# Weights loaded in three parts between the first pairs' x, gate weights in separate tiles: a four-layer graph network on one core

## The chip, the cores and the metric

The kernel runs on one core of one Trainium2 chip. The metric is the device time of one execution in microseconds. Of the kernel before there are six runs: median 1531.78 us, from 1530.32 to 1532.71.

## The reference, cut to what matters

64 graphs of 256 nodes with 128 features go through four layers, each closed by a residual and a layer norm. All is float32. Layer 0, where the change lies, is a gated recurrent unit with five steps:

```python
def step(h, _):
    m_in = jnp.einsum('nm,bmd->bnd', in_matrix, h)
    m_out = jnp.einsum('nm,bmd->bnd', out_matrix, h)
    av = jnp.concatenate([m_in, m_out], axis=-1)
    u3 = h @ u3_w.T + u3_b
    z = jax.nn.sigmoid(av @ w3_w.T + w3_b + u3)
    r = jax.nn.sigmoid(av @ w4_w.T + w4_b + u3)
    hv = jnp.tanh(av @ w5_w.T + w5_b + (r * h @ u5_w.T + u5_b))
    h = (1.0 - z) * h + z * hv
    return (h, None)
...
x = _layernorm(x + _L0_gnn_ref(x, adj, adj, ..., 5), axis=-1)
```

`in_matrix` and `out_matrix` are both `adj`, so the two halves of each gate weight act on the same message and can be added once. The three later layers are an attention over edges that depends on weights only, a graph attention with an isomorphism network, and a Chebyshev filter of order 3.

## The kernel before, in words

The 64 graphs are worked on as 32 pairs. A pair's x is a tile of 128 partitions by 512 columns with nodes on the partitions (class X, 13 buffers); its transpose hT comes from a second array, xT (class T, 3 buffers). The pairs do not depend on each other, so that many are in work at the same time.

One step of layer 0 (`layer0`, L571) is: the **spread**, adjacency times h (`spread`, L484, four matmuls of 256 columns into one bank of PSUM), copied to SBUF (L200); the **reset** gate, u3 times hT (L578) plus w4 times the message (L579), its tanh on ScalarE (L582) and r times h on VectorE (L584); the **z** gate, w3-w4 times the message added onto the same bank (L586), its tanh (L588); the **candidate**, w5 times the message (L593) and u5 times r times h (L594), its tanh (L596); and three VectorE operations for the new h (L598 to L601). The new hT is turned back to nodes on partitions by `turn`: a 32x32 block transpose on VectorE (L465), a store to DRAM on SP's queue (L467) and four reads (L473). A float32 matmul appears in the trace as two records.

The order of all work is set by a planner, `Schedule.order`. It knows for each operation an engine, a duration and how long after its end the result can be used: `seen`, plus LAG, 0.8 us. It takes again and again the operation that could start first, and on equal starts the one that is due first. Then all instructions are issued in that order. Each engine executes its own instructions in that order, and SP issues all DMAs in it. So a wrong figure in the plan doesn't make the kernel wrong; it makes an instruction stand in the queue and wait.

Loads are operations of SP without inputs. `load` (L225) gives each 0.45 us on SP and `seen` of 1.7 + KB/256 us. At the start the loads are, in this order: aT, x0, W0 (the eight matrices of layer 0, 512 KB), hT0, the bias columns, x1, hT1, x2, hT2, the adjacency a, W1 (13 further matrices, 832 KB), the rows. The x and hT of pairs 3 to 31 are added in the loop over pairs; the x go out as soon as one of 13 buffers is free, an hT needs one of 3.

Four matmuls on ones (L253) stand ahead of the first spread. VectorE then adds the halves of the three gate weights into one tile, w345, subtracts w4 from w3 (L260) and halves u5 (L261). The dependencies are kept per tile: whatever reads w345 waits for all writers of w345.

Of the kernel before, what the change touches and what calls it, by code (L numbers as in the profile page):

```python
# [12 lines left out]
P = 128  # L13
N = 256
D = 128
# [8 lines left out]
NEG_MASK = 3.0e38  # L24
NEG_ADJ = 9.0e15

MATS = ["w3a", "w3b", "w4a", "w4b", "w5a", "w5b", "u3", "u5",
        "l1w0", "l1w1", "wp", "wpT", "w1", "w2",
        "v0", "v1", "v2", "v3", "v4", "v5", "v6"]
N_L0 = 8  # L30
COLS = ["w3_b", "u3_b", "w4_b", "w5_b", "u5_b", "bp", "a_src", "a_dst", "mlp_g", "mlp_b", "e0", "e1"]
ROWS = ["l1_bias", "bp", "b1", "gat_g", "gat_b", "b2"]

# [13 lines left out]
def mm(cols):  # L47

    return cols * 0.00168 + 0.005
# [117 lines left out]
def kernel(ctx: ExitStack, tc: tile.TileContext, x, xT, adj, adjT, mats, cols, rows, out):  # L167
    nc = tc.nc
# [5 lines left out]
    S = Schedule(n_pairs)  # L174

    def fixed(shape, name):
        return Value(ap=const.tile([P, *shape], F32, name=name), name=name)

    def pe(us, fn, r, w):
        S.add([("PE", us, fn)], r, w)  # L180

    def act(us, fn, r, w):
        S.add([("ACT", us, fn)], r, w)

    def dve(us, fn, r, w):
        S.add([("DVE", us, fn)], r, w)

    def dve2(us, fn, r, w):
        S.add([("DVE+", us, fn)], r, w)
# [13 lines left out]

    diff, ident = fixed([P], "diff"), fixed([P], "ident")
    aT, a = fixed([2, N], "aT"), fixed([2, N], "a")
    W0, W1 = fixed([N_L0, D], "W0"), fixed([len(MATS) - N_L0, D], "W1")
    ccol = fixed([len(COLS)], "ccol")
    n_rows = len(ROWS) * D + 2
    rbc = fixed([n_rows], "rbc")
# [1 line left out]

    def mat(name):
        i = MATS.index(name)
        return W0.ap[:, i, :] if i < N_L0 else W1.ap[:, i - N_L0, :]

    def col(name):
        i = COLS.index(name)
# [2 lines left out]
    def row(name, n):  # L220
        i = ROWS.index(name)
        return rbc.ap[:, None, i * D:(i + 1) * D].to_broadcast([P, n, D])

    def load(o, i, v, kb=256):
        S.add([("SP", 0.45, lambda: nc.sync.dma_start(o(), i))], [], [v], 1.7 + kb / 256)  # L225

    xs = [Value("X", name=f"x{p}") for p in range(n_pairs)]
    hTs = [Value("T", name=f"hT{p}") for p in range(n_pairs)]

    def load_x(p):  # L230
        load(lambda: xs[p].at(4, D), x[2 * p:2 * p + 2].rearrange("b (t p) d -> p (b t) d", p=P), xs[p])
        load(lambda: hTs[p].at(2, N), xT[2 * p:2 * p + 2].rearrange("b d n -> d b n"), hTs[p])

    pool(1.0, lambda: nc.gpsimd.iota(diff.ap, pattern=[[1, P]], base=0, channel_multiplier=-1,
# [1 line left out]
    dve(0.2, lambda: nc.vector.tensor_scalar(ident.ap, diff.ap, 0.0, None, op0=ALU.is_equal), [diff], [ident])  # L236
    dve(0.1, lambda: nc.vector.memset(neg_half.ap, -0.5), [], [neg_half])
    load(lambda: aT.ap, adjT.rearrange("(t p) i -> p t i", p=P), aT)
    load(lambda: xs[0].at(4, D), x[0:2].rearrange("b (t p) d -> p (b t) d", p=P), xs[0])
    load(lambda: W0.ap, mats[:, :N_L0], W0, 512)  # L240
    load(lambda: hTs[0].at(2, N), xT[0:2].rearrange("b d n -> d b n"), hTs[0])
    load(lambda: ccol.ap, cols, ccol, 16)
    for p in range(1, 3):
        load_x(p)
    load(lambda: a.ap, adj.rearrange("(t p) j -> p t j", p=P), a)
    load(lambda: W1.ap, mats[:, N_L0:], W1, 832)
    load(lambda: rbc.ap, bass.AP(tensor=rows.tensor, offset=rows.offset, ap=[[0, P], [1, n_rows]]), rbc)


# [4 lines left out]

    w345, u5h, bzrh = fixed([3, D], "w345"), fixed([D], "u5h"), fixed([3], "bzrh")
    for i, w in ((1, "w4"), (0, "w3"), (2, "w5")):
        dve(0.25, lambda i=i, w=w: nc.vector.tensor_add(w345.ap[:, i, :], mat(w + "a"), mat(w + "b")), [W0], [w345])
    dve(0.25, lambda: nc.vector.tensor_sub(w345.ap[:, 0, :], w345.ap[:, 0, :], w345.ap[:, 1, :]), [w345], [w345])  # L260
    dve(0.2, lambda: nc.vector.tensor_scalar(u5h.ap, mat("u5"), 0.5, None, op0=ALU.mult), [W0], [u5h])  # L261
    for i, (b, c) in enumerate((("w3_b", "u3_b"), ("w4_b", "u3_b"), ("w5_b", "u5_b"))):
        dve(0.16, lambda i=i, b=b, c=c: nc.vector.tensor_add(bzrh.ap[:, i:i + 1], col(b), col(c)), [ccol], [bzrh])
# [4 lines left out]
    def centre(v, ap, k):  # L268

        m = Value("S", name="mean")  # L270
        mean = lambda: m.at(32)[:, :k]
        dve(0.15 * k + 0.1, lambda: nc.vector.tensor_reduce(mean(), ap(), AX.X, ALU.add), [v], [m])
        dve(0.1, lambda: nc.vector.tensor_scalar(mean(), mean(), -1.0 / D, None, op0=ALU.mult), [m], [m])
        dve(0.15 * k + 0.1, lambda: nc.vector.tensor_add(ap(), ap(), mean().unsqueeze(2).to_broadcast([P, k, D])), [m, v], [v])
# [97 lines left out]
    dve(TT, lambda: nc.vector.tensor_copy(offT.ap, t5.at(2, N)), [t5], [offT])  # L372


    i_w = MATS.index("l1w0") - N_L0
    assert MATS[i_w + N_L0:i_w + N_L0 + 3] == ["l1w0", "l1w1", "wp"] and ROWS[:3] == ["l1_bias", "bp", "b1"]
    centre(W1, lambda: W1.ap[:, i_w:i_w + 3, :], 3)
    i_w1 = MATS.index("w1") - N_L0
    centre(W1, lambda: W1.ap[:, i_w1:i_w1 + 1, :], 1)
    centre(rbc, lambda: rbc.ap[:, :3 * D].rearrange("p (k d) -> p k d", d=D), 3)  # L380
    maskb, ginT, eps1 = fixed([2, N], "maskb"), fixed([2, N], "ginT"), fixed([1], "eps1")
# [60 lines left out]
    def to_sbuf(t, name):  # L442
        v = Value("A", name=name)
        evacuate(lambda: v.at(512), lambda: t.at(512), [t], [v])
        return v
# [32 lines left out]
    def spread(i, right):  # L478

        t = Value("PS", name="ps")  # L480
        for b in range(2):
            def fn(b=b):
                for j in range(2):
                    nc.tensor.matmul(t.at(2, N)[:, b, :], tokens(i)[:, 2 * b + j, :], right.ap[:, j, :],  # L484
                                     start=(j == 0), stop=(j == 1))
            pe(mm(512), fn, [i, right], [t])
        return t
# [35 lines left out]
    def layer_norm(y, o):  # L523
        normalize(y, o, *stats(y))
# [46 lines left out]
    def layer0(x0, hT):  # L571
        h = x0
        for s in range(STEPS):
            mT = to_sbuf(spread(h, aT), "mT")
            t = Value("PS", name="ps")

            def reset(t=t, hT=hT, mT=mT):
                nc.tensor.matmul(t.at(512), mat("u3"), hT.at(512), start=True, stop=False)  # L578
                nc.tensor.matmul(t.at(512), w345.ap[:, 1, :], mT.at(512), start=False, stop=True)  # L579
            pe(mm(1024), reset, [W0, w345, hT, mT], [t])  # L580
            r, z, hv, new = (Value("A", name=n) for n in ("r", "z", "hv", "hT"))
            act(0.59, lambda t=t, r=r: nc.scalar.activation(r.at(512), t.at(512), AF.Tanh, bias=bzrh.ap[:, 1:2], scale=0.5),  # L582
                [t, bzrh], [r])
            dve2(TT, lambda r=r, hT=hT: nc.vector.scalar_tensor_tensor(r.at(512), r.at(512), 1.0, hT.at(512),  # L584
                                                                      op0=ALU.add, op1=ALU.mult), [r, hT], [r])
            pe(mm(512), lambda t=t, mT=mT: nc.tensor.matmul(t.at(512), w345.ap[:, 0, :], mT.at(512), start=False, stop=True,  # L586
                                                            skip_group_check=True), [w345, mT, t], [t])
            act(0.59, lambda t=t, z=z: nc.scalar.activation(z.at(512), t.at(512), AF.Tanh, bias=bzrh.ap[:, 0:1], scale=0.5),  # L588
                [t, bzrh], [z])
            t = Value("PS", name="ps")  # L590

            def candidate(t=t, mT=mT, r=r):
                nc.tensor.matmul(t.at(512), w345.ap[:, 2, :], mT.at(512), start=True, stop=False)  # L593
                nc.tensor.matmul(t.at(512), u5h.ap, r.at(512), start=False, stop=True)  # L594
            pe(mm(1024), candidate, [w345, u5h, mT, r], [t])
            act(0.59, lambda t=t, hv=hv: nc.scalar.activation(hv.at(512), t.at(512), AF.Tanh, bias=bzrh.ap[:, 2:3]),  # L596
                [t, bzrh], [hv])
            dve2(TT, lambda hv=hv, hT=hT: nc.vector.tensor_sub(hv.at(512), hv.at(512), hT.at(512)), [hv, hT], [hv])  # L598
            dve2(TT, lambda hv=hv, z=z: nc.vector.scalar_tensor_tensor(hv.at(512), z.at(512), 1.0, hv.at(512),  # L599
                                                                      op0=ALU.add, op1=ALU.mult), [hv, z], [hv])  # L600
            dve2(TT, lambda hv=hv, hT=hT, new=new: nc.vector.scalar_tensor_tensor(  # L601
                new.at(512), hv.at(512), 0.5, hT.at(512), op0=ALU.mult, op1=ALU.add), [hv, hT], [new])
            hT = new
            h = turn(hT, "h", "h" if s < STEPS - 1 else "y")
        y = Value("A", name="y")
        dve2(TT, lambda: nc.vector.tensor_add(y.at(512), h.at(512), x0.at(512)), [h, x0], [y])
        layer_norm(y, x0)
# [131 lines left out]
    for p in range(n_pairs):  # L739
        S.pair = p  # L740
        if p >= 3:
            load_x(p)
        layer0(xs[p], hTs[p])
        layer1(xs[p])
        layer2(xs[p])
        layer3(xs[p], p)
# [51 lines left out]
```

## Time and profile before

| what | value |
|---|---|
| median of six runs | 1531.78 us |
| time of the profiled execution | 1531.59 us |
| its span | 1529.8 us |
| its mean granted clock of TensorE | 0.998 |
| spread, L484 on x, mean of one record | 385 ns, 512 records |
| gate matmul, L578, mean of one record | 593 ns, 256 records |
| tanh of the reset gate, L582, mean | 687 ns |
| DMA of the whole span | 209.41 MB, 137 GB/s |

The span reaches from the first to the last event of the profile; the execution's own time is 1.8 us longer. A record of a matmul lasts longer than the distance to the next one, since matmuls overlap; where the pace is meant, the text takes the distances between starts. The granted clock is the share of full speed that TensorE was given. A wait is put down to the thing that released it.

### The profile page before, as it was taken

To read this page: it belongs to the slowest core of one execution; us is meant where nothing else is said; L and a number is where in the kernel's file an instruction comes from. 1 tells how busy PE (TensorE), PEld (TensorE's weight loads), DVE (VectorE), ACT (ScalarE), POOL (GpSimd) and SP (SyncE) were. 2 spreads that over 40 slices of the span, in tenths; PEclk is the share of its full clock that TensorE was granted. 3 is DMA by queue.
4 is the path that set the end of the run, shared out by engine and by line. 5 is a ranking of instruction groups with operands and counts; after the bars stand their busy time and mean duration, and the time that the engine had idled before them with its cause. 6 is when DMAs were issued, how large, how long until landed. Compare 5 with 4: busy or idle time off the path is not lost.

```text
span 1529.8 us, 22320 instructions
## 1 busy us (share of the span) xinstructions
PE 1520.2 (99%) x6360; PEld 1060.4 (69%) x6360; DVE 1170.0 (76%) x2880; ACT 901.7 (59%) x2403; POOL 353.6 (23%) x446
## 2 busy tenths in 40 slices
PE   9999999999999999999999999999999999999998
PEld 5555666666767667766666676766677777778997
DVE  5566767788987887777877777876888788988964
ACT  3443545556656665566665566655566457767963
POOL 0000001112221222221221212221132232235552
PEclk9999999999999999999999999999999999999999
DMA  7534556767886767667767677686778666854631
GB/s 220 110 75 97 104 115 140 154 134 156 169 160 141 159 140 147 141 137 168 150 130 153 139 154 155 141 152 125 146 151 169 136 143 142 167 100 91 139 84 42
DMA packets 912506, 209.41 MB, mean 137 GB/s; under 512 B 698496, under 2 KB 907904, under 8 KB 912384
## 3 DMA queue, kind: packets, MB, share of 16 engines
q1 hardware_dynamic: 912384, 207.99, 65.4%
q8 instruction: 51, 0.84, 0.2%
q14 instruction: 71, 0.58, 0.1%
HBM read 113.45 MB, written 94.44 MB: 136 GB/s over the span
## 4 chain that ended last, share of the span: by engine, by line
PE 97%; DMA 1%; ACT 1%; SPq 0%; DVE 0%; issue 0%; POOL 0%; POOLq 0%; DVEq 0%; ACTq 0%
PE ps L484 28%; PE ps L593 9%; PE ps L578 9%; PE ps L594 9%; PE ps L586 9%; PE ps L579 9%; PE ps L615 7%; PE ps L684 4%; PE ps L730 4%; PE ps L722 3%; PE ps L723 3%; PE ps L643 2%; PE ps L459 1%; DMA x<-x_in 0%; DMA a<-d 0%
## 5 line engine op out<-in xcount | busy, mean ns | idle before, releaser
L200 ACT COPY a<-ps 128x512 f32<-128x512 f32 (+1 forms) x312 | 169.7, 546 | 184.7 <-PE ps L484 136.1
L484 PE MATMUL ps<-aT,a 128*128 128x256 f32 x1024 | 241.4, 379 | 0.0
L484 PEld LDWEIGHTS ps<-aT,a 128*128 128x128 f32 x1024 | 193.7, 190 | 63.0 <-issue 39.2
L582 ACT ACTIVATE a<-ps,bzrh 128x512 f32<-128x512 f32 x160 | 109.9, 687 | 172.7 <-PE ps L579 170.9
L596 ACT ACTIVATE a<-ps,bzrh 128x512 f32<-128x512 f32 x160 | 109.8, 686 | 166.8 <-PE ps L594 163.5
L547 POOL TENSOR_SCALAR s<-s 128x4 f32<-128x4 f32 x96 | 42.6, 444 | 622.1 <-DVE s L538 326.2
L593 PE MATMUL ps<-a,w 128*128 128x512 f32 x320 | 163.6, 593 | 0.0
L594 PE MATMUL ps<-a,u5h 128*128 128x512 f32 x320 | 163.4, 592 | 0.0
L579 PE MATMUL ps<-a,w 128*128 128x512 f32 x320 | 163.4, 592 | 0.0
L586 PE MATMUL ps<-a,w 128*128 128x512 f32 x320 | 163.3, 592 | 0.0
L588 ACT ACTIVATE a<-ps,bzrh 128x512 f32<-128x512 f32 x160 | 109.9, 687 | 77.3 <-PE ps L586 74.5
L615 PEld LDWEIGHTS ps<-W,a 128*128 128x128 f32 x1024 | 127.9, 192 | 28.0 <-issue 26.5
L599 DVE SCALAR_TENSOR_TENSOR a<-a,a 128x512 f32<-128x512 f32 x160 | 110.4, 690 | 47.0 <-ACT a L588 43.7
L550 POOL TENSOR_TENSOR s<-s,neg_half 128x4 f32<-128x4 f32 x128 | 139.5, 1090 | 10.4
L465 DVE STREAM_TRANSPOSE a<-a 128x512 f32<-128x512 f32 x181 | 128.0, 708 | 5.9 <-ACT a L561 0.3
L578 PE MATMUL ps<-a,W 128*128 128x512 f32 x256 | 130.8, 593 | 0.0
L615 PE MATMUL ps<-W,a 128*128 128x128 f32 x1024 | 129.3, 275 | 0.0
L484 PE MATMUL ps<-aT,x 128*128 128x256 f32 x512 | 126.8, 385 | 1.8 <-DMA x<-x_in 1.8
L598 DVE TENSOR_TENSOR a<-a,a 128x512 f32<-128x512 f32 x128 | 88.7, 694 | 46.5 <-ACT a L596 45.4
L484 PEld LDWEIGHTS ps<-aT,x 128*128 128x128 f32 x512 | 97.1, 194 | 32.4 <-issue 19.3
L579 PEld LDWEIGHTS ps<-a,w 128*128 128x128 f32 x320 | 60.8, 190 | 76.5 <-issue 68.6
L594 PEld LDWEIGHTS ps<-a,u5h 128*128 128x128 f32 x320 | 60.7, 190 | 76.6 <-issue 59.3
(183 smaller groups left out, 2670.4 us busy)
## 6 DMA issues: line engine op xcount, KB each, us to landing
e<-a SPq DMA_DIRECT2D x268, 256.0 KB
a<-e SPq DMA_DIRECT2D x1072, 64.0 KB
e<-b SPq DMA_DIRECT2D x30, 512.0 KB
b<-e SPq DMA_DIRECT2D x120, 128.0 KB
x<-x_in SPq DMA_DIRECT2D x32, 256.0 KB
t<-xT_in SPq DMA_DIRECT2D x32, 256.0 KB
a<-d SPq DMA_DIRECT2D x32, 256.0 KB
y_out<-a SPq DMA_DIRECT2D x32, 256.0 KB
```

Source lines behind the costliest of these rows:

```text
L200: S.add([("ACT", us[0], lambda: nc.scalar.copy(o(), i())), ("DVE", us[1], lambda: nc.vector.tensor_copy(o(), i()))], r, w)
L465: dve(n / 512 * 0.55 + 0.09, lambda: nc.vector.transpose(st.at(n), i.at(n)), [i], [st])
L484: nc.tensor.matmul(t.at(2, N)[:, b, :], tokens(i)[:, 2 * b + j, :], right.ap[:, j, :], start=(j == 0), stop=(j == 1))
L550: pool(1.02, lambda: nc.gpsimd.tensor_tensor(rs(), rs(), neg_half.ap, op=ALU.pow), [s, neg_half], [s])
L578: nc.tensor.matmul(t.at(512), mat("u3"), hT.at(512), start=True, stop=False)
L579: nc.tensor.matmul(t.at(512), w345.ap[:, 1, :], mT.at(512), start=False, stop=True)
L582: act(0.59, lambda t=t, r=r: nc.scalar.activation(r.at(512), t.at(512), AF.Tanh, bias=bzrh.ap[:, 1:2], scale=0.5), [t, bzrh], [r])
L586: pe(mm(512), lambda t=t, mT=mT: nc.tensor.matmul(t.at(512), w345.ap[:, 0, :], mT.at(512), start=False, stop=True, skip_group_check=True), ...
L593: nc.tensor.matmul(t.at(512), w345.ap[:, 2, :], mT.at(512), start=True, stop=False)
L594: nc.tensor.matmul(t.at(512), u5h.ap, r.at(512), start=False, stop=True)
L599: dve2(TT, lambda hv=hv, z=z: nc.vector.scalar_tensor_tensor(hv.at(512), z.at(512), 1.0, hv.at(512), op0=ALU.add, op1=ALU.mult), [hv, z], ...
L615: nc.tensor.matmul(tokens(t)[:, c, :], tokens(i)[:, c, :], w(), start=(k == 0), stop=(k == len(lefts) - 1))
```

## The change

MATS is reordered, so that w4a, w4b and u3 come first. The matrices are loaded in three parts: Wg (w4a, w4b, u3; 192 KB), W0 (w3, w5, u5; 320 KB) and W1 (the rest; 832 KB). The start's loads are now aT, x0, x1, Wg, hT0, columns, W0, hT1, x2, hT2, a, W1, rows. w345 becomes three tiles, w3, w4, w5. The planner's figure for how long a load takes until its tile can be used depends on what was added before it. On each engine the matmuls, activations and vector operations are as many as before; SP issues one DMA more. Lines from `load` on are 6 to 13 higher than before: the spread is L497, the reset gate L591 and L592, z L599, the candidate L606 and L607.

```diff
-MATS = ["w3a", "w3b", "w4a", "w4b", "w5a", "w5b", "u3", "u5",
+MATS = ["w4a", "w4b", "u3", "w3a", "w3b", "w5a", "w5b", "u5",
...
-N_L0 = 8
+PARTS = (0, 3, 8, len(MATS))
...
-    W0, W1 = fixed([N_L0, D], "W0"), fixed([len(MATS) - N_L0, D], "W1")
+    Wg, W0, W1 = (fixed([e - b, D], f"W{b}") for b, e in zip(PARTS, PARTS[1:]))
...
+    loads = []
+
     def load(o, i, v, kb=256):
-        S.add([("SP", 0.45, lambda: nc.sync.dma_start(o(), i))], [], [v], 1.7 + kb / 256)
+
+        loads.append(kb)
+        n = len(loads)
+        S.add([("SP", 0.45, lambda: nc.sync.dma_start(o(), i))], [], [v], max(2.7, 2.2 + sum(loads) / 245 - 0.45 * n) if n < 24 else 2.7)
...
     load(lambda: aT.ap, adjT.rearrange("(t p) i -> p t i", p=P), aT)
-    load(lambda: xs[0].at(4, D), x[0:2].rearrange("b (t p) d -> p (b t) d", p=P), xs[0])
-    load(lambda: W0.ap, mats[:, :N_L0], W0, 512)
-    load(lambda: hTs[0].at(2, N), xT[0:2].rearrange("b d n -> d b n"), hTs[0])
+    def load_w(k, v):
+        load(lambda: v.ap, mats[:, PARTS[k]:PARTS[k + 1]], v, 64 * (PARTS[k + 1] - PARTS[k]))
+    load_x(0)
+    load_x(1)
+    load_w(0, Wg)
+    load_h(0)
     load(lambda: ccol.ap, cols, ccol, 16)
-    for p in range(1, 3):
-        load_x(p)
+    load_w(1, W0)
+    load_h(1)
+    load_x(2)
+    load_h(2)
     load(lambda: a.ap, adj.rearrange("(t p) j -> p t j", p=P), a)
-    load(lambda: W1.ap, mats[:, N_L0:], W1, 832)
+    load_w(2, W1)
...
-    for i, w in ((1, "w4"), (0, "w3"), (2, "w5")):
-        dve(0.25, lambda i=i, w=w: nc.vector.tensor_add(w345.ap[:, i, :], mat(w + "a"), mat(w + "b")), [W0], [w345])
-    dve(0.25, lambda: nc.vector.tensor_sub(w345.ap[:, 0, :], w345.ap[:, 0, :], w345.ap[:, 1, :]), [w345], [w345])
+    for v, w, part in ((w4, "w4", Wg), (w3, "w3", W0), (w5, "w5", W0)):
+        dve(0.25, lambda v=v, w=w: nc.vector.tensor_add(v.ap, mat(w + "a"), mat(w + "b")), [part], [v])
+    dve(0.25, lambda: nc.vector.tensor_sub(w3.ap, w3.ap, w4.ap), [w3, w4], [w3])
...
-            pe(mm(1024), reset, [W0, w345, hT, mT], [t])
+            pe(mm(1024), reset, [Wg, w4, hT, mT], [t])
...
         if p >= 3:
             load_x(p)
+            load_h(p)
```

The z gate and the candidate read w3 and w5 in the same manner. On the host the matrices are stacked in the new order.

More of the change, by code (lines that the diff above doesn't have):

```diff
@@ L213, in mat @@
         i = MATS.index(name)
-        return W0.ap[:, i, :] if i < N_L0 else W1.ap[:, i - N_L0, :]
+        return next(w.ap[:, i - b, :] for w, b, e in zip((Wg, W0, W1), PARTS, PARTS[1:]) if i < e)
     def col(name):
@@ L231, in load_x, with load_h @@
         load(lambda: xs[p].at(4, D), x[2 * p:2 * p + 2].rearrange("b (t p) d -> p (b t) d", p=P), xs[p])
+    def load_h(p):
         load(lambda: hTs[p].at(2, N), xT[2 * p:2 * p + 2].rearrange("b d n -> d b n"), hTs[p])
@@ L253 @@
         pe(0.87, lambda: nc.tensor.matmul(idle.at(N), ones.ap[:, :P], ones.ap, start=True, stop=True), [ones], [idle])
-    w345, u5h, bzrh = fixed([3, D], "w345"), fixed([D], "u5h"), fixed([3], "bzrh")
-    for i, w in ((1, "w4"), (0, "w3"), (2, "w5")):
-        dve(0.25, lambda i=i, w=w: nc.vector.tensor_add(w345.ap[:, i, :], mat(w + "a"), mat(w + "b")), [W0], [w345])
-    dve(0.25, lambda: nc.vector.tensor_sub(w345.ap[:, 0, :], w345.ap[:, 0, :], w345.ap[:, 1, :]), [w345], [w345])
+    w3, w4, w5, u5h, bzrh = fixed([D], "w3"), fixed([D], "w4"), fixed([D], "w5"), fixed([D], "u5h"), fixed([3], "bzrh")
+    for v, w, part in ((w4, "w4", Wg), (w3, "w3", W0), (w5, "w5", W0)):
+        dve(0.25, lambda v=v, w=w: nc.vector.tensor_add(v.ap, mat(w + "a"), mat(w + "b")), [part], [v])
+    dve(0.25, lambda: nc.vector.tensor_sub(w3.ap, w3.ap, w4.ap), [w3, w4], [w3])
     dve(0.2, lambda: nc.vector.tensor_scalar(u5h.ap, mat("u5"), 0.5, None, op0=ALU.mult), [W0], [u5h])
@@ L372 @@
     dve(TT, lambda: nc.vector.tensor_copy(offT.ap, t5.at(2, N)), [t5], [offT])
-    i_w = MATS.index("l1w0") - N_L0
-    assert MATS[i_w + N_L0:i_w + N_L0 + 3] == ["l1w0", "l1w1", "wp"] and ROWS[:3] == ["l1_bias", "bp", "b1"]
+    i_w = MATS.index("l1w0") - PARTS[2]
+    assert MATS[i_w + PARTS[2]:i_w + PARTS[2] + 3] == ["l1w0", "l1w1", "wp"] and ROWS[:3] == ["l1_bias", "bp", "b1"]
     centre(W1, lambda: W1.ap[:, i_w:i_w + 3, :], 3)
-    i_w1 = MATS.index("w1") - N_L0
+    i_w1 = MATS.index("w1") - PARTS[2]
     centre(W1, lambda: W1.ap[:, i_w1:i_w1 + 1, :], 1)
@@ L578, in reset @@
                 nc.tensor.matmul(t.at(512), mat("u3"), hT.at(512), start=True, stop=False)
-                nc.tensor.matmul(t.at(512), w345.ap[:, 1, :], mT.at(512), start=False, stop=True)
-            pe(mm(1024), reset, [W0, w345, hT, mT], [t])
+                nc.tensor.matmul(t.at(512), w4.ap, mT.at(512), start=False, stop=True)
+            pe(mm(1024), reset, [Wg, w4, hT, mT], [t])
             r, z, hv, new = (Value("A", name=n) for n in ("r", "z", "hv", "hT"))
@@ L585, in layer0 @@
                                                                       op0=ALU.add, op1=ALU.mult), [r, hT], [r])
-            pe(mm(512), lambda t=t, mT=mT: nc.tensor.matmul(t.at(512), w345.ap[:, 0, :], mT.at(512), start=False, stop=True,
-                                                            skip_group_check=True), [w345, mT, t], [t])
+            pe(mm(512), lambda t=t, mT=mT: nc.tensor.matmul(t.at(512), w3.ap, mT.at(512), start=False, stop=True,
+                                                            skip_group_check=True), [w3, mT, t], [t])
             act(0.59, lambda t=t, z=z: nc.scalar.activation(z.at(512), t.at(512), AF.Tanh, bias=bzrh.ap[:, 0:1], scale=0.5),
@@ L592, in candidate @@
             def candidate(t=t, mT=mT, r=r):
-                nc.tensor.matmul(t.at(512), w345.ap[:, 2, :], mT.at(512), start=True, stop=False)
+                nc.tensor.matmul(t.at(512), w5.ap, mT.at(512), start=True, stop=False)
                 nc.tensor.matmul(t.at(512), u5h.ap, r.at(512), start=False, stop=True)
-            pe(mm(1024), candidate, [w345, u5h, mT, r], [t])
+            pe(mm(1024), candidate, [w5, u5h, mT, r], [t])
             act(0.59, lambda t=t, hv=hv: nc.scalar.activation(hv.at(512), t.at(512), AF.Tanh, bias=bzrh.ap[:, 2:3]),
@@ L770 @@
     mats = []
-    for w in (L0_gnn_w3_w, L0_gnn_w4_w, L0_gnn_w5_w):
-        wT = np.asarray(w).T
-        mats += [wT[:D], wT[D:]]
-    mats += [np.asarray(L0_gnn_u3_w).T, np.asarray(L0_gnn_u5_w).T]
+    halves = lambda w: [np.asarray(w).T[:D], np.asarray(w).T[D:]]
+    mats += [*halves(L0_gnn_w4_w), np.asarray(L0_gnn_u3_w).T]
+    mats += [*halves(L0_gnn_w3_w), *halves(L0_gnn_w5_w), np.asarray(L0_gnn_u5_w).T]
     mats += [np.asarray(L1_gnn_W)[0], np.asarray(L1_gnn_W)[1]]
```

## The prediction

> **What bounds the kernel now.** I read the page's busy times first, then the table of waits of TensorE, then its timeline from the start, then stretches of equal behaviour.
>
> ```profile
> span 1529.8 us, 22320 instructions
> PE 1520.2 (99%) x6360; PEld 1060.4 (69%) x6360; DVE 1170.0 (76%) x2880; ACT 901.7 (59%) x2403; POOL 353.6 (23%) x446
> ```
>
> TensorE is busy for all but 9.6 us. Its waits say where the rest is:
>
> ```profile
> PE ps L484 <- DMA x<-x_in: 1.8, 1, 1.8
> PE ps L253 <- DVE ones L251: 1.2, 1, 1.2
> PE ps L722 <- DVE s L665: 0.3, 1, 0.3
> ```
>
> One wait matters, and it is at the start: the spread of pair 1 waits for x1. The timeline of TensorE (start, duration, count) and the stretches (busy time, granted clock, DMA share, GB/s) show what else that wait costs:
>
> ```profile
> 1.20 3.78 PE L253 MATMUL ps<-ones 128*128 128x256 f32 x8 [1.20 <-DVE ones L251]
> 4.78 2.84 PE L484 MATMUL ps<-aT,x 128*128 128x256 f32 x8
> 9.46 4.54 PE L484 MATMUL ps<-aT,x 128*128 128x256 f32 x12 [1.84 <-DMA x<-x_in]
> 13.84 1.02 PE L578 MATMUL ps<-t,W 128*128 128x512 f32 x2
> ...
> 7.60:9.46 1.86, 0.02 (x1) 1.00 1.13 347
> 9.46:13.84 4.38, 4.38 (x12) 0.61 1.05 373
> 20.00:1448.00 1428.00, 1428.00 (x5908) 1.00 0.68 139
> ```
>
> At full clock one 256-column record follows the last after 0.216 us, a 512-column one after 0.429 us (distances between starts in the trace; each matmul is two records). The first spread would let the next start at 7.46; it starts at 9.46: 2.0 us lost. The clock record then has half speed from 10.10 to 13.52, so 12 records worth 2.59 us take 4.38: 1.79 us more. From 20 to 1448 us TensorE never stops. **So the start can give back 3.8 us at most, and any microsecond that TensorE loses anywhere is a microsecond of the span.**
>
> Who is late is read on the queue of SP and in VectorE's waits for loads:
>
> ```profile
> 1.72 0.50 SPq L225 DMA_DIRECT2D W<-mats_in  x1
> 3.25 0.43 SPq L225 DMA_DIRECT2D x<-x_in  x1
> 8.87 11.63 SPq L225 DMA_DIRECT2D x<-x_in  x10
> 12.55 0.43 DVE L288 TENSOR_SCALAR a<-a 128x512 f32<-128x512 f32 x1 [2.25 <-DMA a<-adj_in]
> 16.39 0.55 DVE L272 TENSOR_REDUCE s<-rbc 128x3 f32<-128x384 f32 x1 [2.10 <-DMA rbc<-rows_in]
> 16.40:21.40 5.00, 5.00 (x17) 2.96 (x16) 4.83 (x17) 2.01 (x4) 0.00 (x0) 1.00 0.97 259
> ```
>
> x1 is the sixth load, behind the 512 KB of W0. Then the ten further x are issued in one run from 8.87, and the DMA engines are full (share 0.97) until 21.4. The completion counts of the trace put the last of 16 increments at 9.42 for x1, 16.36 for the rows, then 17.23, 18.07, 18.88, 19.71, 20.59, **21.42** for x3 to x8. The increments of W0 reach twelve by 6.19 and sixteen at 7.70.
>
> **What the skill says.** (1) The Trainium skill, "TensorE: Matmul & The Clock Gate", section "What's actually happening": TensorE's clock falls to half after an idle window of about 3.4 us that runs freely, and comes back after a busy one. The trace agrees on the length (half clock for 3.41 us), but an idle time of only 1.84 us sufficed. (2) The same page, "Step-by-step: what each phase is for": matmuls stay in program order. The trace agrees: nothing is pulled ahead of the waiting spread from 7.6 to 9.46. (3) "DMA: Bandwidth & Descriptors", "Why a DMA increments its semaphore by 16 and not by 1": only the full 16 means that all has landed. So the slowest engine counts, as with W0 above.
>
> **The change part by part.**
>
> *Loads reordered.* aT, x0 stay first; x1 becomes third, then Wg (192 KB), h0, columns, W0 (320 KB), h1, x2, h2. x1 now has 512 KB before it instead of 1286: x0 has landed at 4.36, and one 256 KB load takes about 0.84 us (the steps from 17.23 to 21.42), so x1 lands near 5.2, at worst 2.1 us later if W0's delay falls on it; it is needed at 7.46. The 2.0 us go. Next late: h0 with Wg is needed at 9.19 and has 1216 KB up to its end, less than what had landed by 8.70 before (the columns). h1 and x2 have the same bytes before them as now and land at 10.20 and 11.06, needed at 10.90 and 12.62. All are in time, the tightest by 0.5 to 0.7 us.
>
> *Three tiles.* The same sums on VectorE (0.28 us each); w4 no longer waits for the other gates. w3 is ready after W0's 320 KB, at about 9.4 plus four operations, 10.5; it is needed at 14.34. Worth nothing beyond the reset of pair 0 being able to start early, which is counted here. One more DMA is issued, 0.45 us on SP, which waits for completions anyway: nothing; its cover gone, 0.45 us.
>
> *The planner's new figure for a load.* This is what the change moves. `load` now expects max(2.7, 2.2 + KB so far/245 - 0.45 n) us for the first 23 loads that the program adds, 2.7 after them. The program adds 13 loads at the start, then x and h by turns, so x3 is n=14 (11.9 us), x7 is n=22 (3664+9x256=5968 KB: 16.7 us), and **x8 is n=24: 2.7 us**. But on SP the h wait for buffers, and the x go out one after another: x8 is the 19th DMA, behind everything. The planner believes it there at 19x0.46+2.7+0.8=12.3 us (0.45 us an issue with its margin of 1.03, LAG 0.8) and so ahead of x3 to x7. The instruction order of the changed kernel shows the consequence: TensorE's 14th row, right after pair 0's z matmul, is half of the spread of the tile that the 19th DMA fills, waiting for that DMA. (In the kernel before, the row in this place takes x3, the 13th DMA.)
>
> TensorE in that order: first spread to 7.46; spread of pair 1, 8x0.216, to 9.19; resets of pairs 0 and 1, 2x4x0.429, to 12.62; spread of pair 2 to 14.34; z of pair 0, 0.86, to **15.20**. Then it waits for x8. Up to x8 the bytes are those of before, so it lands at 21.4 to 21.5: **6.3 us lost**. Behind it stand the candidates of pairs 0 and 1, z of pair 1 and all that follows; ScalarE and VectorE run dry behind them. Bounds: at the highest rate of a 5 us stretch (374 GB/s at 7.6 to 12.6) the 5.45 MB through x8 take 14.6 us from 2.6, so 17.2 at the earliest, 2.0 us lost; with a second delay like W0's (2.1), 23.5, 8.3 us. I take 21.5, the measured landing.
>
> *The clock after it.* A wait of some 6 us leaves a window with little work wherever the windows fall; before, one with 46% work (1.57 of 3.41 us) was enough. After resuming, TensorE stays at half speed until a window was busy enough (61% in the first one, 1.2 to 3.28, was not). With the windows' position open, I estimate 2.3 to 5.7 us at half speed, losing 1.1 to 2.9 us; I take 2.0. Before it was 1.79.
>
> *Later.* From TensorE's row 188 of 2268, some 160 us in (adding up the rows by the distances above), the order equals that of before, tail included; there nothing waits. In between the first turned tile is needed at row 40. It is shifted as TensorE is: counting durations of before (candidate 1.7, tanh 0.9, four VectorE operations 2.8 each for two pairs, 5.4 us from issue of the four reads to landing), it is ready about 15 us after resuming, needed 17.9 after. So 0 us, up to 2 if this fails.
>
> **Sum**, against the profiled execution (1531.59, span 1529.8): -2.0 - 1.8 + 6.3 + 2.0 = **+4.5: 1536.1**. The median 1531.78 lies 0.2 above it: **1536.3**.
>
> **Rivals.** (a) *The change does what it says*: the row 14 load isn't late, or its wait is for another load. -3.8: **1528.0**. Against it: the landing at 21.42 is measured and x8 is still last. It decides if x8 lands before 15.2; the fastest bound is 17.2. 4%. (b) *The delay of W0 goes with its split*: the four slow engines carry it from 7.7 to all later loads; if smaller rows avoid it, x8 lands 2.1 earlier, 19.4. The stall is 4.2, and -3.8+4.2+1.5 to 2.0 gives +1.9 to +2.4: **1533.9**, not slower by the bound below. It decides from a landing before 20.1. For it: W0 took 3.3 us, x0 0.84. Against: the large W1 had no such delay, so it may belong to the first reads of the matrices, which Wg then meets. 16%. (c) *A second stall*: the turned tiles of pairs 0 and 1 miss rows 40 and 43, since SP issues in order and the store of pair 1 stands before the reads of pair 0. +2 to 4: **1539.5**. For: its slack is under 3 us. Against: that chain moves with TensorE, and the planner left no such wait from 20 to 1448 us. 8%. (d) The forecast: 72%.
>
> **Chances.** 0.2% is 3.06 us, about what a measurement of this kernel can tell from no change. Slower by more: (d) and (c), 0.80. Within: most of (b), 0.16. Faster: (a), 0.04. The range takes 17.2+ for the landing out as unlikely, 19 to 22.5 in, with 1.1 to 2.9 for the clock: 1533.2 to 1539.0.
>
> **What would show it.** Right: TensorE has one wait for an x load of 5 to 7 us near 15 us, at the spread's line (L497 then), none near 7.6; half clock soon after it; no idle time from 30 us to the tail. Wrong: a start without a gap, x8 landing before 19 us, or waits for transposed tiles near 40 us. If the landing holds and the total doesn't, the clock's term was the mistake.

## The result and the profile after

The changed kernel takes 1535.84 us (median of 18 runs, 1534.29 to 1536.53), the kernel before 1531.79 us (38 runs, 1529.55 to 1532.78). The ratio is 1.0027, with a 95% interval from 1.0020 to 1.0033: **4.05 us slower**. The profiled execution took 1535.76 us.

The page of the changed kernel, its span and busy times:

```profile
span 1533.9 us, 22323 instructions
PE 1520.7 (99%) x6360; PEld 1060.0 (69%) x6360; DVE 1171.5 (76%) x2880; ACT 901.5 (59%) x2403; POOL 354.5 (23%) x446
```

The span has grown by 4.1 us, TensorE's busy time by 0.5: the time lies in waits. TensorE's waits (engine, line, released by; us in total, times, longest):

```profile
PE ps L497 <- DMA x<-x_in: 4.8, 1, 4.8
PE ps L266 <- DVE ones L264: 1.2, 1, 1.2
PE ps L735 <- DMA a<-e: 0.7, 2, 0.5
```

Again there is one wait for an x, but 4.8 us in place of 1.8. TensorE's timeline says which one (start, duration, count):

```profile
4.78 4.65 PE L497 MATMUL ps<-aT,x 128*128 128x256 f32 x16
9.27 1.02 PE L591 MATMUL ps<-t,W 128*128 128x512 f32 x2
...
14.43 1.02 PE L599 MATMUL ps<-a,w 128*128 128x512 f32 x2
20.23 1.92 PE L497 MATMUL ps<-aT,x 128*128 128x256 f32 x4 [4.79 <-DMA x<-x_in]
21.94 1.91 PE L606 MATMUL ps<-a,w 128*128 128x512 f32 x2
```

The stretch after the wait (its length, TensorE's busy time, granted clock, DMA share, GB/s):

```profile
20.20:23.86 3.66, 3.63 (x7) 0.53 0.78 186
```

The first two spreads run as one group of sixteen records: the wait for x1 near 7.6 us is gone. After the z matmul at 14.43 comes the new one, at the half spread (four records) of pair 8, which starts at 20.23; x8's last increment is at 20.19. The clock record has half speed from 20.43 to 23.84. Two loads, read on VectorE's timeline, show where the DMAs stand:

```profile
6.96 0.29 DVE L272 TENSOR_TENSOR w<-W 128x128 f32<-128x128 f32 x1 [2.75 <-DMA W<-mats_in]
11.67 0.43 DVE L301 TENSOR_SCALAR a<-a 128x512 f32<-128x512 f32 x1 [2.22 <-DMA a<-adj_in]
```

Wg is complete at 6.93 and the adjacency at 11.65 (12.53 before), and x3 to x8 complete at 15.67, 16.58, 17.48, 18.38, 19.29 and 20.19: each 0.9 us apart (0.8 to 0.9 before), but 1.2 to 1.6 us sooner than before.

Adding up how much later than at full speed each record starts, the kernel before loses 4.76 us between 4.78 and 30 us, the changed one 7.77 us: 3.0 more. From 200 us on they lose 0.86 and 1.82, small waits most of which lie near 1437 to 1453 us: 1.0 more. The way from the last matmul to the end is 0.2 longer. That is the 4.1 us of the spans.

### The profile page after: what moved, and what is told of

Same layout as the page of the kernel before. It is cut to its first block, busy times and chain, and to the rows that moved or that the text cites. A ratio compares the mean times of both kernels' runs of the same rounds, so it can differ in the third digit from the quotient of the medians.

```text
span 1533.9 us, 22323 instructions
## 1 busy us (share of the span) xinstructions
PE 1520.7 (99%) x6360; PEld 1060.0 (69%) x6360; DVE 1171.5 (76%) x2880; ACT 901.5 (59%) x2403; POOL 354.5 (23%) x446
## 4 chain that ended last, share of the span: by engine, by line
PE 96%; DMA 2%; SPq 1%; ACT 0%; DVE 0%; issue 0%; POOLq 0%; DVEq 0%; POOL 0%; ACTq 0%
PE ps L497 28%; PE ps L606 9%; PE ps L607 9%; PE ps L599 9%; PE ps L591 9%; PE ps L592 9%; PE ps L628 7%; PE ps L697 4%; PE ps L735 3%; PE ps L736 3%; PE ps L743 3%; PE ps L656 2%; SPq L231 1%; PE ps L472 1%; DMA a<-e 0%; DMA x<-x_in 0%
## 5 line engine op out<-in xcount | busy, mean ns | idle before, releaser
L497 PE MATMUL ps<-aT,a 128*128 128x256 f32 x1024 | 241.3, 379 | 0.0
L497 PEld LDWEIGHTS ps<-aT,a 128*128 128x128 f32 x1024 | 193.7, 190 | 62.2 <-issue 39.0
L606 PE MATMUL ps<-a,w 128*128 128x512 f32 x320 | 164.4, 595 | 0.0
L607 PE MATMUL ps<-a,u5h 128*128 128x512 f32 x320 | 163.5, 592 | 0.0
L592 PE MATMUL ps<-a,w 128*128 128x512 f32 x320 | 163.4, 592 | 0.0
L599 PE MATMUL ps<-a,w 128*128 128x512 f32 x320 | 163.3, 592 | 0.0
L497 PE MATMUL ps<-aT,x 128*128 128x256 f32 x512 | 126.3, 384 | 4.8 <-DMA x<-x_in 4.8
L591 PE MATMUL ps<-a,W 128*128 128x512 f32 x256 | 130.8, 592 | 0.0
L497 PEld LDWEIGHTS ps<-aT,x 128*128 128x128 f32 x512 | 96.1, 192 | 35.2 <-issue 19.3
L607 PEld LDWEIGHTS ps<-a,u5h 128*128 128x128 f32 x320 | 61.0, 191 | 77.1 <-issue 61.8
L592 PEld LDWEIGHTS ps<-a,w 128*128 128x128 f32 x320 | 60.8, 190 | 76.5 <-issue 68.9
```

Source lines behind the costliest of these rows:

```text
L592: nc.tensor.matmul(t.at(512), w4.ap, mT.at(512), start=False, stop=True)
L606: nc.tensor.matmul(t.at(512), w5.ap, mT.at(512), start=True, stop=False)
```

## The experiments

Theory A is that of the prediction: the new figure makes the planner expect x8 far too early, TensorE stands for its landing and runs at half clock after it. Theory B is that the other things the change does (load order, one DMA more, finer tiles, another row order on TensorE) cost the time.

### The planner's figure up to the 33rd load

```diff
-        ... if n < 24 else 2.7)
+        ... if n < 34 else 2.7)
```

> The changed kernel, with the planner's new figure kept up to the 33rd load in place of the 23rd, so that every x of the first run of loads has it. TensorE's row 14 is then the square of the adjacency, whose load landed at 11.65 us, in place of the spread of the tile that the 19th DMA fills; the load order and the three tiles stay. Theory A (the whole loss is the wait for that load and the half clock after it): no wait of TensorE for an x, no half clock after the first, 3.8 us less than the kernel before: 1528.0 (1527.3 to 1529.0), ratio 0.9975. Theory B (the new order of the loads, the extra DMA or the finer tiles cost the time): still about 1535.8, ratio 1.0027. Theory C (the wait goes, but another load or a turned tile is late in its place): one wait of 1 to 3 us for x or a turned tile, 1529 to 1532.

Measured: 1528.23 us, ratio 0.9974 (0.9964 to 0.9983). The waits of TensorE in this kernel, all of them:

```profile
PE ps L266 <- DVE ones L264: 1.2, 1, 1.2
```

And the stretch from the first spread to 24 us:

```profile
4.40:24.00 19.60, 19.60 (x64) 1.00 1.09 315
```

No wait for a load is left, and TensorE is busy throughout. It runs at full clock from 6.26 us on, where the clock record begins; before that the column's 1.00 says nothing, and the records of the first spread start 0.427 us apart, half the pace, as in every kernel here. Load order, the extra DMA and separate tiles are still in it, so these parts of theory B are out as the cause. The row order of the changed kernel is not in it; that part is decided below, with one DMA moved. This kernel beats both others: 3.9 us less than the kernel before (1532.14 on the same chip) and 8.0 less than the changed one, adding the two distances from the kernel before.

### The old figure, new loads and tiles

```diff
-        ..., max(2.7, 2.2 + sum(loads) / 245 - 0.45 * n) if n < 24 else 2.7)
+        ..., 1.7 + kb / 256)
```

> The changed kernel with the planner's old figure for a load, 1.7 us plus KB/256: only the order of the loads and the separate tiles are left of the change. Its TensorE takes the spread of pair 2 right after that of pair 1, at 9.2 us, where x2 landed at 10.28 in the changed kernel. Theory A: a wait of about 1.1 us for that x2, half clock after it for one window or not (0 to 1.7 us): 1531.8 - 3.8 + 1.1 + 0 to 1.7 = 1529.1 to 1530.8. Theory B (loads and tiles cost the time): 1535 or more.

Measured: 1530.48 us, ratio 0.9991 (0.9982 to 0.9999). TensorE's waits:

```profile
PE ps L497 <- DMA x<-x_in: 1.6, 1, 1.6
PE ps L266 <- DVE ones L264: 1.2, 1, 1.2
PE ps L735 <- DVE s L678: 0.2, 1, 0.2
```

TensorE's order is, row by row, that of the kernel before; what changed is when loads land. The wait is now for x2 and takes 1.6 us, and no half clock follows in this profile. So the loads and tiles by themselves are a small gain, 1.7 us less than before on the same chip, and the figure decides whether more of it (the experiment before this) or a loss comes out.

### Idle matmuls in the wait

```diff
+        late = next(op for op, fn in order if op.ways[0][0] == "PE" and xs[8] in op.reads)
...
+            if op is late:
+                for _ in range(10):
+                    nc.tensor.matmul(idle.at(N), ones.ap[:, :P], ones.ap, start=True, stop=True)
```

> The changed kernel with ten matmuls of 256 columns on the tile of ones, into the bank of the warm-up, placed before the late spread: TensorE has 4.3 us of idle work while it waits for x8, and nothing else differs. Theory A, with the clock as a part of the loss: the spread still starts when x8 lands (near 20.2), no half clock after it: 1.6 to 1.7 us less than the changed kernel, about 1534.2, ratio to the kernel before 1.0016. If the half clock cost nothing in the total: as the changed kernel, 1535.8. If the filler work delays something: more than 1536.

Measured: 1534.21 us, ratio 1.0017 (1.0011 to 1.0024). TensorE's timeline around the place:

```profile
14.24 1.02 PE L599 MATMUL ps<-a,w 128*128 128x512 f32 x2
15.10 4.48 PE L774 MATMUL ps<-ones 128*128 128x256 f32 x20
20.27 1.13 PE L497 MATMUL ps<-aT,x 128*128 128x256 f32 x4 [0.70 <-DMA x<-x_in]
21.24 1.02 PE L606 MATMUL ps<-a,w 128*128 128x512 f32 x2
```

The late spread starts when it did, at 20.27, but it takes 1.13 us in place of 1.92, and the clock record has no half speed. The clock's share is the difference of the ratios, 0.0010 of 1532 us: 1.5 us (by the medians 2.0, 4.05 less 2.07; the intervals of the two ratios overlap, so the totals alone bound it loosely). The profiles say 1.70: the changed kernel loses 1.80 us against full speed from 20.23 to 30 us, and 0.10 of it, at the first record after the wait, stands here too, at full clock. The wait itself remains.

### One DMA moved on SP

All computing engines keep the changed kernel's order. x8 is issued before x3:

```diff
+        at = lambda p: next(k for k, (op, _) in enumerate(order) if xs[p] in op.writes and op.ways[0][0] == "SP")
+        late = order.pop(at(8))
+        order.insert(at(3), late)
...
```

> The changed kernel with one DMA moved on SP: the load of x8 is issued before that of x3 (as the 14th DMA) in place of after that of x7 (19th). The order on TensorE, VectorE, ScalarE and GpSimd is that of the changed kernel to the row, the early spread of pair 8 included. The 14th DMA landed at 14.8 us in the changed kernel, and the spread is reached at 15.3. Theory A (the landing of this one tile is the loss): no wait, no half clock, 1528.0 to 1529.5, ratio 0.997 to 0.9985. Theory B (the order on TensorE costs it, through later waits): 1534 or more.

Measured: 1529.10 us, ratio 0.9982 (0.9976 to 0.9989). Its late spread:

```profile
15.39 1.13 PE L497 MATMUL ps<-aT,x 128*128 128x256 f32 x4 [0.46 <-DMA x<-x_in]
```

x8 completes at 15.35, TensorE waits 0.46 us, and 7.1 us are back (3.0 under the kernel before in place of 4.05 over it). The order on TensorE, which theory B blames, is untouched. The counterpart, with `order.insert(at(12) + 1, late)`:

> The counterpart: the load of x8 is issued after that of x12, as the 23rd DMA, which landed at 23.64 us in the changed kernel; all orders of the four computing engines are those of the changed kernel. Theory A: wait 8.4 us in place of 4.95, half clock for one to two windows after it: 1535.8 + 3.4 + 0 to 1 = 1539.2 (1538 to 1541). If an early spread's delay sets off later waits like those of the kernel whose figure went up to the 29th load (1552.65): above 1545. Then its 16 us would come from the delay and not from the other order at the end.

Measured: 1539.29 us, ratio 1.0054 (1.0041 to 1.0068).

Its timeline around the late spread:

```profile
23.34 2.08 PE L497 MATMUL ps<-aT,x 128*128 128x256 f32 x4 [8.14 <-DMA x<-x_in]
25.20 1.84 PE L606 MATMUL ps<-a,w 128*128 128x512 f32 x2
```

The wait follows the landing of this one tile in both directions, and the total follows the wait: the late spread starts 3.1 us later than in the changed kernel, and the span is 3.2 us longer.

### The figure up to the 19th and the 29th load

`n < 20` puts the tile of x6 in row 14, `n < 30` that of x11.

> The changed kernel with the planner's new figure up to the 19th load in place of the 23rd: the first x that it wrongly expects after 2.7 us is x6, the 17th DMA, in place of x8, the 19th; TensorE's order up to row 13 and the place of the late spread (row 14) are the same. x6 landed at 18.38 us in the changed kernel, x8 at 20.19, and row 14 is reached at 15.3. Theory A (the wait is for the landing of the misjudged tile): wait 3.1 us in place of 4.95, and half clock after it for a window or not (0 to 1.7 us): 1528.2 + 3.1 + 0 to 1.7 + up to 1.0 of small late waits = 1531.3 to 1534.0, most likely 1533.3. Theory B (a row order with an early spread costs this whatever the tile): as the changed kernel, 1535.8.

Measured: 1533.26 us, ratio 1.0009 (1.0001 to 1.0018), from 1531.06 to 1534.97 over its runs. The wait in the profile is 3.3 us, with no half clock after it:

```profile
14.56 1.02 PE L599 MATMUL ps<-a,w 128*128 128x512 f32 x2
18.85 1.13 PE L497 MATMUL ps<-aT,x 128*128 128x256 f32 x4 [3.26 <-DMA x<-x_in]
```

The profiled execution took 1531.58 us, 1.7 less than the median. That most of the others had the half clock after the wait would fit, but no profile of one was taken.

> The same with the figure up to the 29th load: the tile in row 14 is that of the 22nd DMA (x11), which landed at 22.87 us in the changed kernel. Theory A: wait 7.6 us, half clock for about one window after it: 1528.2 + 7.6 + 1.7 + 0.5 to 1.0 = 1538.0 to 1538.5 (range 1537 to 1540). Theory B: 1535.8.

Measured: **1552.65 us**, ratio 1.0135 (1.0120 to 1.0151): some 14 us above the 1538.0 to 1538.5 expected, a miss. The five longest waits of its TensorE:

```profile
PE ps L497 <- DMA x<-x_in: 7.1, 1, 7.1
PE ps L697 <- DMA b<-e: 3.5, 1, 3.5
PE ps L497 <- ACT x L532: 3.2, 1, 3.2
PE ps L628 <- DVE a L640: 2.1, 2, 1.1
PE ps L266 <- DVE ones L264: 1.2, 1, 1.2
```

The first line is as expected: 7.1 us, then half clock to 27.90. The next three lie between 1410 and 1530 us. The reason is in the order of the instructions: in the changed kernel and in the one with `n < 20` the order on TensorE is that of the kernel before from row 188 on (177 and 174 us in their traces), in this one only in the last two rows. The planner has found another course, and its end has turned tiles and norms that come late, with half clock from 1441.02 to 1444.43 and from 1526.35 to 1533.18. That it isn't the delay is shown by the kernel with x8 issued last: 8.14 us of wait with the changed kernel's order, 1539.29, no such waits. What within the new order is late was not followed further.

### The split of the weights alone

In the kernel before, the 512 KB come in two DMAs (192 and 320 KB) in their old place, with the matrices stacked in the new order.

```diff
-    load(lambda: W0.ap, mats[:, :N_L0], W0, 512)
+    load(lambda: W0.ap[:, :N_G], mats[:, :N_G], W0, 512)
+    load(lambda: W0.ap[:, N_G:], mats[:, N_G:N_L0], W0, 512)
...
```

> The kernel before with its 512 KB of W0 loaded by two DMAs (192 and 320 KB) in the place of the one, into the same tile; order, planner's figure for each part as for the 512 KB, and the rest as before. It tells whether it was the split that let x8 land 1.2 us earlier in the changed kernel than in the kernel before. If the split does it: x1 lands near 8.1 to 8.6 in place of 9.42, the wait of TensorE near 7.6 shrinks from 1.84 us to 0.6 to 1.1: 1530.5 to 1531.2. If the early landing was by chance or by x1 being ahead of the weights: x1 lands at 9.2 to 9.8, 1531.8 to 1532.2.

And the kernel before once more, for a second profile:

> The kernel before, unchanged, for a second profile. It tells whether the late completion of its 512 KB of weights (7.70 us, the last of four slow engines) is a property of that transfer or of that execution. If of the transfer: x1 lands again at 9.2 to 9.8, the wait near 7.6 is again 1.7 to 2.2 us. If of that execution: W0 completes near 6.8, x1 lands at 8.3 to 8.7, the wait is 0.7 to 1.1 us, as in the kernel with W0 split in place.

In the two profiles of the kernel before, the weights complete 3.34 and 3.65 us after x0, x1 at 9.42 and 9.71. With the split they complete 2.40 us after x0, x1 at 8.47. So the delay belongs to the one large transfer, not to one execution, and the split takes about 1 us of it away. It is also what brings x8 forward: with the split alone x8 completes at 20.14, in the changed kernel at 20.19, in the two profiles of the kernel before at 21.41 and 21.54. TensorE's wait near 7.6 in the second profile of the kernel before:

```profile
PE ps L484 <- DMA x<-x_in: 2.2, 1, 2.2
```

And with the split:

```profile
PE ps L485 <- DMA x<-x_in: 0.7, 1, 0.7
```

In time the gain that was expected isn't seen: 1531.82 us, ratio 0.9997 (0.9989 to 1.0006), for 1530.5 to 1531.2. The profiled execution took 1530.40, the fastest of its 13, whose slowest took 1532.98; what the others lose was not seen.

### One tile for the gates again

The kernel of the first experiment with w345 back:

```diff
-            pe(mm(1024), reset, [Wg, w4, hT, mT], [t])
+            pe(mm(1024), reset, [Wg, w345, hT, mT], [t])
...
```

> The kernel of the first experiment (new figure up to the 33rd load, no late spread) with the three gate weights back in one tile, so that every reader of one gate waits for all sums. In the first experiment the second half of the first reset is reached at 9.83 us, and the sums of all gates are done at about 9.5 (W0 8.08, four operations of 0.28). Theory A (the separate tiles are worth nothing by themselves once x1 comes first): no wait, 1528.2 (1527.5 to 1529.2). If the separate tiles are what lets TensorE run through: a wait of VectorE of 0.3 us or more near 9.8, 1528.6 to 1530.

Measured: 1527.55 us, ratio 0.9972 (0.9962 to 0.9983), no wait of TensorE but that of the warm-up. With the one tile the planner also takes another order on TensorE: row 14 is now the first of three small matmuls (L309). So it is tiles and order together that show no loss; the separate tiles are not needed for the gain. What helps is x1 ahead of the weights, with an order that doesn't reach a load before it has landed.

### All together

Loss: start distances of TensorE's records beyond full speed, from 4.78 to 30 us, plus the 4.32 us of idle matmuls where they are. The rest is the span less this loss. In every kernel the first spread starts at half clock, until 5.36 to 7.42 us in these profiles; that part, 0.3 to 1.3 us of each loss, differs from execution to execution. The medians come from several chips, on which the kernel before took 1531.6 to 1532.1.

| kernel | median us | span of the profile | loss at the start | rest |
|---|---|---|---|---|
| before | 1531.79 | 1529.8 | 4.76 | 1525.0 |
| before, second profile | 1531.64 | 1530.5 | 5.04 | 1525.5 |
| changed | 1535.84 | 1533.9 | 7.77 | 1526.2 |
| figure to the 33rd load | 1528.23 | 1525.9 | 0.73 | 1525.2 |
| the same, one tile | 1527.55 | 1525.8 | 0.83 | 1525.0 |
| old figure | 1530.48 | 1528.3 | 2.79 | 1525.5 |
| idle matmuls in the wait | 1534.21 | 1532.4 | 6.13 | 1526.2 |
| weights split in place | 1531.82 | 1528.6 | 2.92 | 1525.7 |
| figure to the 19th load | 1533.26 | 1529.8 | 4.70 | 1525.1 |
| x8 issued first | 1529.10 | 1526.7 | 1.24 | 1525.4 |
| x8 issued last | 1539.29 | 1537.1 | 10.90 | 1526.2 |
| figure to the 29th load | 1552.65 | 1551.6 | 11.20 | 1540.4 |

In eleven of twelve profiles the rest is the same to 1.3 us, while the losses at the start go from 0.73 to 10.90: most of the difference between these kernels lies in the first 30 us (3.0 of the changed kernel's 4.1). The twelfth has another order to its end.

## Why the prediction was right

It gave 1536.3 (1533.2 to 1539.0) and the median is 1535.84: 4.05 us of loss for 4.5 forecast. By its steps:

- **x1 in time.** Right: the second spread starts without a gap, and h0, Wg, h1 and x2 are all there when needed. The next wait is row 14's.
- **The misjudged load.** Right, and shown by moving that DMA alone: 1529.10 when it comes before x3, 1539.29 when it comes after x12. Rival (a), that the wait isn't for a late load, is refuted by this.
- **The size of the wait.** 6.3 us forecast, 4.95 measured (in distances of starts). The term was the landing of x8, taken as 21.5 from the kernel before; it was 20.19. The step that failed is "up to x8 the bytes are those of before, so it lands at 21.4 to 21.5": the bytes are the same, their time isn't. Rival (b) had named the cause: the delay of W0 goes with its split. It gave 2.1 us, the profiles show 1.2 at x8 (1.3 with the split alone). Its own edge for the landing was 20.1, so x8 came 0.1 us later than it needed.
- **The clock.** 2.0 us forecast, 1.80 in the profile, counted as the prediction counts the 1.79 of before; 1.70 of it is the clock's own, 1.5 to 2.0 by the idle matmuls. The bound, 1.1 to 2.9, held.
- **Later.** Between 30 and 200 us nothing waits, so rival (c) didn't come: the first turned tile is used at 39.91, on time. But "0 us" for the end was 1.0 us too low: the profile has 1.82 us of small waits after 200 us in place of 0.86, though the order is the same. The kernel before has 0.86 and 1.28 in its two profiles, so nearly half of it lies within what executions differ by. The rest may belong to the late start: the kernels with idle matmuls and with x8 last have 1.9 there too, those with `n < 20` and x8 first 0.7 and 1.1, all with the same order at the end. Why was not followed.

So the total came closer than its terms: -1.35 for the wait, -0.2 for the clock, +1.0 at the end and +0.2 after the last matmul. That these partly cancel is luck. Without the 1.0 us at the end the total would be some 3.1 us, on the edge of the 3.06 that the prediction took for no change. The one thing that the forecast didn't see at all is how little protects the tail: it took the return to the old order from row 188 as a fact of this kernel, rightly, but the kernel with `n < 30` shows that a neighbouring figure doesn't return and pays 15 us.

## What to carry to other kernels

When an order is planned ahead, a figure for one load matters only against the figures of its neighbours: an estimate that gets better up to a cut and falls back to an old value behind it makes the last in the queue look like the first. After a change to such a figure, look first at the order that comes out: which instruction on the bound engine is the first to wait for a load far back in the queue, and whether the tail is still the old one. Both can be read before anything runs, and each microsecond of such a wait is paid in full where one engine is busy 99% of the time.

## What the runs showed of the hardware

A wait's length doesn't by itself say whether the clock falls. Idle times of 1.84 and 2.20 us near 8 us (the kernel before, twice) and of 4.79, 7.11 and 8.14 us were followed by half clock; those of 0.7 and 1.6 us were not, and neither was the 3.26 us of the kernel with `n < 20`, whose runs spread over 3.9 us. The Trainium skill, "TensorE: Matmul & The Clock Gate", section "What's actually happening", speaks of an idle window of about 3.4 us; here 1.84 us sufficed and 3.26 us didn't.

The clock records show a fixed grid: in each profile all changes of the clock lie whole multiples of 3.413 us apart (with `n < 30` the fall at 1441.02 comes 414 of them after the rise at 27.90), and where the grid lies differs from execution to execution. But a window's busy share by itself doesn't decide either: cut by this grid, windows busy for 46 and 36% (the kernel before, twice) were followed by half clock, windows with 44% (`n < 30`) and with 48 and 57% (`n < 20`, the wait of 3.26 us) were not. What else counts was not settled.

One DMA of 512 KB in rows of 4 KB completed 3.3 to 3.7 us after the load before it, the same bytes in two DMAs with rows of 1.5 and 2.5 KB 2.4 us after it; yet the 832 KB in rows of 6.5 KB, issued later, took 2.1 us in both kernels. Whether the first reads of the matrices or the rows cause it was not tried.
